# A gated block's third pair started a round later, the second expert block's groups cut 4, 2, 2, and the dealing begun with the lead-in round

## The chip, the cores and the metric

The kernel runs on one core of one Trainium2 chip. The metric is the device time of one execution in microseconds (us); of several runs the median is given. Engines are named as the profile names them: PE multiplies matrices (PEld is its weight loading), DVE and ACT work elementwise, POOL issues the row scatters and small powers, SP issues the plain DMAs.

## The reference

Eight sequences of 512 positions and 128 channels go through a chain of blocks, each added to its input after a layer norm. What matters here is the end of the chain:

```python
x = x + attention(layernorm(x))     # L1_attn_a, softmax over 16 heads
x = x + experts(layernorm(x))       # L1_ffn, first block ("m" in the kernel)
x = x + gated(layernorm(x))         # L1_attn_b, gated linear attention
x = x + experts(layernorm(x))       # L1_ffn again, second block ("n")

def experts(x):                     # top 2 of 8 experts per position
    xn = rms_norm(x)
    scores = xn @ w_router.T
    ids = top_k(scores, 2);  c = softmax(scores)[ids]
    h = val * silu(gate)            # val, gate = xn @ w_up[e].T, 352 wide each
    return sum(c * (h @ w_down[e].T)) + x
```

The gated block is a scan along the positions of one sequence, with projections, a short convolution, a series for a logarithm, and matrix products over chunks of 128 positions.

## The kernel before

**Expert blocks.** Positions are sorted by expert. A block works in *groups* of sequences (`GROUPS`, L26: one tuple for each block). For a group of `seqs` sequences there are 4 x `seqs` token tiles of 128 positions and `tiles_of(seqs)` slots of 128 rows: 39 for four sequences, 23 for two. The steps of a group are: `steps` (norms and router scores, for each sequence), `choose` (L1038 on: top 2, softmax, and for each row its slot; chains of small DVE instructions, with two matmuls at L1073 and L1074), scatters of the rows to `slots` in DRAM (L1159, one for each token tile and choice), `tiles` (L1189 on), scatters of the results to `given` (L1171, one for each slot tile), and `combine` (L1296 on: loads of `y` from `given`, and `add`, whose weighted additions into `x` are L1324).

The scatters are dealt by the generator `posts`, one at each call; it prefers rows to `slots` unless five results wait. A group's first load from `slots` waits for all its scatters, and a `y` load waits for all of the group's results.

A slot tile in `tiles` is: two products with `w_up` (L1274, L1275), a tanh on ACT (L1280), two multiplications on DVE (L1287, L1288), three transposes (L1238), their copy (L1240), the product with `w_down` (L1247) and its copy to `yr` (L1250). Four slot tiles share one load (`xr`, L1207) and one transposing step `turned` (L1218, L1220). `tiles` yields once after the first loads and then once for each slot tile and two more: a group of 39 takes 42 such *pieces*.

**Gated block.** It works on four *pairs* of sequences. `gated_steps` (L1573 on) cuts a pair's work into 25 steps, to which four steps of the second expert block's norms and scores are added (`steps` in `gated_and_experts`). `pipeline` (L54) runs the pairs in *rounds*. A round is the list `ages` of 29 places; an entry a means "the next step of the pair that started a rounds ago". There are 2 places with age -1 (the norm; places 15 and 22), 15 with age 0 (the first transposes L1630 to the product at L1768), 8 with age 1 (chunk products from L1776 to the sum into `x`, L1845) and 4 with age 2 (the expert norms and scores). So a pair's first step is its norm in the round ahead of its own, and round -1 holds the norm of pair 0 alone.

**What is dealt beside the pairs.** After each place from round `first` on, `pipeline` takes one step of `side`, a table of streams and the steps at which each is called (`dealt`). `at(now, places)` gives the steps `(now + 1) * 29 + place`. In the table `first` and `last` are the first block's two groups, `before.tiles(last)` the 42 pieces of its second group, `posts` its scatters; `one`, `two` and `three` are the second block's groups, `own` its scatters, and `tiles` their pieces one group after the other. After the rounds `run(side)` calls what is left of the table, and then `blend` runs the remaining pieces (`left`), scatters and combines in the *tail*.

The order in which the program is written is the order in which PE, DVE, ACT and POOL run it (`in_program_order`); only scatters of one set are loose among themselves.

Of the kernel before, what the change touches and what calls it, by code (L numbers as in the profile page):

```python
# [20 lines left out]
B = 8  # L21
# [1 line left out]
D = 128  # L23
NT = S // P

GROUPS = ((4, 4), (2, 4, 2))  # L26
MOST = max(max(g) for g in GROUPS)


# [24 lines left out]
def pipeline(make, count, ages, side=None, every=0, first=0):  # L54

    live = {}
    done = 0
    for now in range(min(ages), count + max(ages)):  # L60
        for age in ages:
            n = now - age
            if 0 <= n < count:
                if n not in live:
                    live[n] = make(n)
                next(live[n], None)
            done += 1
            if side is not None and now >= first and done % every == 0:
                next(side, None)
# [5 lines left out]
@contextmanager  # L75
def in_program_order(tc, *loose):


    block = tc.nc.cur_bb
    first = len(block.bb.instructions)  # L80
    yield
    assert tc.nc.cur_bb is block
    engines = (mybir.EngineType.PE, mybir.EngineType.DVE, mybir.EngineType.Activation, mybir.EngineType.Pool)
    last = {}
    for i in block.bb.instructions[first:]:
        if i.engine in engines:
            group = next((one[i.name] for one in loose if i.name in one), None)
            before = last.setdefault(i.engine, {})
            for other, names in before.items():
                if group is None or other != group:  # L90
                    for name in names:
                        tc.add_manual_dep(i, name, ORDER, reason="the order in which it is written")
            if group is None:
                before.clear()
            before.setdefault(group, []).append(i.name)
# [805 lines left out]
def blend(*streams):  # L901


    live = [[iter(one), 0, n] for one, n in streams]
    while live:
        one = min(live, key=lambda l: (l[1] + 1) / l[2])
        one[1] += 1
        if next(one[0], live) is live:
            live.remove(one)
# [426 lines left out]
def run(stream):  # L1336
    for _ in stream:
        pass


def fast(stream, *many):

    while True:
        for n in many:
            for _ in range(n):
                if next(stream, stream) is stream:
                    return
            yield


def idle(many):
    yield from range(many)
# [10 lines left out]
def until(true):  # L1363

    while not true():
        yield


def whole(stream):

    for _ in stream:
        pass
    yield


def dealt(*streams):

    streams = [(iter(stream), set(steps)) for stream, steps in streams]
    for q in range(1 + max(max(steps) for _, steps in streams)):
        for stream, steps in streams:  # L1380
            if q in steps:
                next(stream, None)
        yield
# [7 lines left out]
def in_turn(m):  # L1391


    streams = [(m.tiles(g), turns(g) - (g.number > 0)) for g in m.groups]

    def pieces():
        for i, (stream, n) in enumerate(streams):
            for at in range(n):
                if at == n - 3 and i + 1 < len(streams):
                    next(streams[i + 1][0])  # L1400
                next(stream)
                yield

    return pieces(), sum(n for _, n in streams)
# [75 lines left out]
def gated_and_experts(k, before, posts, slots, keep, banks, out):  # L1480

    tc = k.tc
    first, last = before.groups
    with tc.tile_pool(name="moe1", bufs=1, side="right") as room:
        m = Experts(k, "n", slots, keep, room, before.p3, out)
        m.hids = before.hids
        one, two, three = m.groups
        tiles, pieces = in_turn(m)
        own = m.posts(sum(2 * g.n + g.tiles for g in m.groups))
        with tc.tile_pool(name="gla1", bufs=1) as alone, tc.tile_pool(name="gla", bufs=2) as pool:  # L1490
            with k.banks(**banks["gated"]):
                gated = gated_steps(k, alone, pool)

                def steps(pair):
                    yield from gated(pair)
                    for _ in zip(m.steps(2 * pair), m.steps(2 * pair + 1)):
                        yield

                ages = (0, 0, 1, 0, 1, 1, 0, 2, 1, 1, 0, 2, 0, 2, 0, -1, 1, 0, 2, 0, 0, 1, -1, 0, 1, 0, 0, 0, 0)

                def at(now, *places):
                    return [(now + 1) * len(ages) + i for i in places]

                side = dealt(  # L1510
                    (before.tiles(last), at(-1, 4, *range(7, 29)) + at(0, *range(0, 29, 2)) + at(1, *range(4))),
                    (posts, at(-1, *range(29)) + at(0, *range(29)) + at(1, *range(6))),
                    (posts, at(-1, *range(9))),
                    (whole(posts), at(1, 6)),
                    (before.combine(first), at(-1, *range(9, 18))),
                    (before.combine(last), at(1, *range(8, 15), 17, 19)),
                    (m.choose(one), at(2, *range(19, 29)) + at(3, *range(3))),
                    (own, at(3, *range(3, 29)) + at(4, *range(29)) + at(5, *range(32))),
                    (own, at(5, *range(0, 32, 2))),
                    (tiles, at(3, *range(20, 29, 2)) + at(4, *range(0, 29, 4)) + at(5, *range(0, 32, 4))),  # L1520
                    (fast(m.choose(two), 2), at(4, *range(19, 26))),
                    (m.choose(three), at(5, *range(19, 32))),
                )
                with in_program_order(tc, before.loose, m.loose):
                    pipeline(steps, B // 2, ages, side=side, every=1)
                    run(side)
        with k.banks(**banks["experts"]), in_program_order(tc, m.loose):
            left = pieces - 21

            def combined(g):  # L1530
                yield from until(lambda: len(g.back) == g.tiles)
                yield from idle(3)
                yield from m.combine(g)

            blend((tiles, left), (take(fast(own, 1, 2), left), left), (chain(*(combined(g) for g in m.groups[:2])), left))
            run(own)
            run(m.combine(three))
# [556 lines left out]
def net_kernel(ctx: ExitStack, tc: tile.TileContext, drams, offsets, out):  # L2094
# [38 lines left out]
    w_a.close()  # L2133
    slots = [blank_slots(k, one) for one in GROUPS]
    with k.banks(**usual):
# [40 lines left out]
    with tc.If(large > 0):  # L2176
        nc.sync.dma_start(flat, saved)
        slots = [blank_slots(k, one) for one in GROUPS]
        again = ExitStack()
# [228 lines left out]
```

## Time and profile before

| | |
|---|---|
| median of 3 runs | 2065.78 us (2059.05 to 2067.45) |
| the profiled execution | 2068.02 us |
| its span | 2066.3 us |
| mean granted TensorE clock | 0.903 of full |
| busy: PE, PEld, DVE, ACT, POOL | 85%, 57%, 62%, 46%, 35% of the span |

A stretch of the profile is read by its window: the busy time of each engine in it, with the number of instructions in brackets, and the TensorE clock that was granted there. Matmuls are pipelined and their ends are modelled, so a PE that is busy all the time may still be below its peak. Durations are those of one execution. Some matmul records can be missing.

### The profile page before, as it was taken

How to read it: one execution, taken by the hardware profiler on the slowest of the kernel's cores; microseconds unless marked ns; L12 is line 12 of the kernel's file. 1: busy time of each engine (PE TensorE's matmuls, PEld its weight loads, DVE VectorE, ACT ScalarE, POOL GpSimd, SP SyncE). 2: the span in 40 equal slices, each digit the busy share in tenths (PEclk: the TensorE clock that was granted, in tenths of full speed). 3: DMA queues.
4: the chain of work that ended last, by engine and by line, in shares of the span. 5: the costliest groups of instructions: out<-in, count | busy, mean ns of one | idle time of the engine just before them, and what ended most of it. 6: DMA issues, size and time to landing. Idle time of an engine off the chain costs nothing. (4 is left out here: it accounts for less than half of the span.)

```text
span 2066.3 us, 29976 instructions
## 1 busy us (share of the span) xinstructions
PE 1751.9 (85%) x10171; PEld 1184.3 (57%) x10171; DVE 1287.4 (62%) x4211; ACT 943.7 (46%) x1703; POOL 731.0 (35%) x866
## 2 busy tenths in 40 slices
PE   4998789999998698899998878868898886847995
PEld 2655577887876455344444446645565654635774
DVE  7644888888886763565667456335746766434554
ACT  1022556666654322465555544434545553413553
POOL 2111333333333521344443663632212103355532
PEclk9898899999998888899999889978999787878998
DMA  9800000000000200000000021121101000112332
GB/s 256 148 1 1 0 1 1 1 1 1 1 1 1 90 1 41 1 1 1 1 1 1 22 70 36 54 75 43 32 10 33 21 1 12 47 41 69 93 103 65
DMA packets 79390, 71.25 MB, mean 34 GB/s; under 512 B 6560, under 2 KB 73120, under 8 KB 78336
## 3 DMA queue, kind: packets, MB, share of 16 engines
q1 hardware_dynamic: 69120, 47.89, 9.3%
q0 software_dynamic: 9536, 20.47, 3.0%
q8 instruction: 86, 1.41, 0.3%
q10 hardware_dynamic: 576, 0.90, 0.1%
q14 instruction: 72, 0.59, 0.1%
HBM read 34.98 MB, written 34.25 MB: 34 GB/s over the span
## 5 line engine op out<-in xcount | busy, mean ns | idle before, releaser
L165 POOL TENSOR_TENSOR ln_rs<-rs_v,mhalf 128x4 f32<-128x4 f32 x144 | 150.8, 1048 | 431.2 <-DVE rs_v L164 418.6
L1171 POOL DMA_INDIRECT given<-yr,to x163 | 160.0, 982 | 345.6 <-ACT yr L1250 105.5
L1287 DVE SCALAR_TENSOR_TENSOR half<-half,ps_a 128x352 f32<-128x352 f32 x163 | 84.6, 519 | 222.8 <-ACT half L1280 179.7
L679 ACT ACTIVATE pr<-ps_s 128x1024 f32<-128x1024 f32 x160 | 154.7, 1018 | 120.8 <-PE ps_s L669 120.7
L1275 PE MATMUL ps_a<-w_m,xt 128*128 x326 | 135.3, 499 | 34.8 <-DVE half L1287 22.4
L1274 PE MATMUL ps_a<-w_m,xt 128*128 x326 | 137.2, 505 | 19.8 <-ACT xt L1220 7.9
L1159 POOL DMA_INDIRECT slots<-xn,rpos x128 | 124.7, 974 | 74.2 <-issue 35.6
L669 PE MATMUL ps_s<-qm,rot 32*128 32x128 f32 (+3 forms) x1024 | 124.8, 490 | 23.6 <-ACT pr L679 23.5
L683 POOL TENSOR_SCALAR_AFFINE_SELECT pr<-pr 128x256 f32<-128x256 f32 x256 | 100.2, 416 | 111.5 <-ACT pr L679 107.2
L530 PEld LDWEIGHTS ps_c<-w_e,mlp_g 128*128 128x128 f32 x1024 | 126.6, 198 | 15.1 <-issue 14.8
L1240 ACT COPY gt<-ps_b 128x384 f32<-128x384 f32 x163 | 78.1, 479 | 112.9 <-PE ps_b L1238 85.2
L530 PE MATMUL ps_c<-w_e,mlp_g 128*128 128x128 f32 x1024 | 128.8, 281 | 0.1
L522 PE MATMUL ps_a<-zt,w_e 128*128 128x512 f32 x256 | 123.7, 607 | 0.9 <-ACT zt L211 0.9
L1280 ACT ACTIVATE half<-ps_a 128x352 f32<-128x352 f32 x163 | 75.9, 466 | 90.3 <-PE ps_a L1274 73.4
L1275 PEld LDWEIGHTS ps_a<-w_m,xt 128*128 128x128 f32 x326 | 63.7, 204 | 83.9 <-DVE half L1287 32.8
L178 DVE BATCH_NORM_AGGREGATE ln_mv<-ln_st 128x2 f32<-128x6 f32 x576 | 100.3, 179 | 16.3
L669 PEld LDWEIGHTS ps_s<-qm,rot 32*128 32x128 f32 x1024 | 60.2, 195 | 82.2 <-ACT pr L679 55.6
L523 ACT ACTIVATE mlp_g<-ps_a,w_col 128x512 f32<-128x512 f32 x128 | 85.8, 687 | 35.4 <-PE ps_a L522 35.4
L224 POOL TENSOR_TENSOR xe<-xe,w_erow 128x512 f32<-128x512 f32 x64 | 82.3, 1306 | 55.2 <-DVE ks L480 54.9
L1238 PEld LDWEIGHTS ps_b<-w_ident,hid 128*128 128x128 f32 x489 | 63.7, 147 | 65.0 <-issue 29.4
L373 ACT ACTIVATE mlp_g<-ps_a,w_col 128x512 f32<-128x512 f32 x64 | 44.0, 687 | 123.9 <-PE ps_a L372 123.2
L1288 DVE SCALAR_TENSOR_TENSOR hid<-half,ps_a 128x352 f32<-128x352 f32 x163 | 85.0, 521 | 18.8 <-PE ps_a L1274 1.1
(385 smaller groups left out, 4054.3 us busy)
## 6 DMA issues: line engine op xcount, KB each, us to landing
xr<-slots SPq DMA_DIRECT2D x37, 260.0 KB
y<-given SPq DMA_DIRECT2D x32, 256.0 KB
slots<-blank SPq DMA_DIRECT2D x3, 2535.0 KB
w_m<-in_m_dram SPq DMA_DIRECT2D x2, 2244.0 KB
w_e<-in_e_dram SPq DMA_DIRECT2D x2, 1700.0 KB
slots<-blank SPq DMA_DIRECT2D x2, 1495.0 KB
given<-yr,to POOLq DMA_INDIRECT x163
x<-in_u_dram SPq DMA_DIRECT2D x8, 256.0 KB
```

Of the source, the lines that this page charges most:

```text
L165: nc.gpsimd.tensor_tensor(out, v, self.mhalf[:, :n], ALU.pow)
L178: nc.vector.bn_aggr(mv[:, t, :], st[:, t, :])
L522: nc.tensor.matmul(ph, w1[:, c * P : (c + 1) * P], ht, start=True, stop=True)
L523: nc.scalar.activation(g[:, c, :], ph, AF.Relu, bias=col["e_b1"][:, l, c : c + 1])
L530: nc.tensor.matmul(py[:, t, :], g[:, c, t * P : (t + 1) * P], w2[:, c, :], start=(c == 0), stop=(c == 3))
L669: nc.tensor.matmul(halves[g // 2][:, g % 2, at : at + S - u * P], kr[rows, u * P : (u + 1) * P], qm[rows, i, u * P : S], start=True, stop= ...
L679: nc.scalar.activation(pr, sc, AF.Exp)
L683: nc.gpsimd.affine_select(out=v, in_=v, pattern=[[0, 2], [1, P]], compare_op=ALU.is_ge, fill=0.0, base=0, channel_multiplier=-1,)
L1159: made = nc.gpsimd.indirect_dma_start(out=g.slots, out_offset=bass.IndirectOffsetOnAxis(ap=g.pos[:, i, t : t + 1], axis=0), in_=g.xn[:, t, :],
L1171: made = nc.gpsimd.indirect_dma_start(out=g.given, out_offset=bass.IndirectOffsetOnAxis(ap=to, axis=0), in_=yr, in_offset=None,)
L1274: nc.tensor.matmul(pg, xt, w["experts"][:, bass.ds(o + HID, HID)], start=True, stop=True)
L1275: nc.tensor.matmul(pv, xt, w["experts"][:, bass.ds(o, HID)], start=True, stop=True)
```

## The change

- `GROUPS` for the second block goes from (2, 4, 2) to (4, 2, 2) sequences: 39, 23 and 23 slot tiles in place of 23, 39 and 23. Group `one` then holds pairs 0 and 1, `two` pair 2, `three` pair 3.
- `pipeline` takes a list of rounds in which pairs start. Pairs start in rounds 0, 1, 3 and 4 in place of 0, 1, 2 and 3, so there is one round more.
- `first=-1`: the dealing begins with round -1 in place of round 0. `at(now, ...)` therefore falls in round `now`; before it fell in round `now + 1`.
- The table of what is dealt is written anew.

By rounds as they run (p0a1 is pair 0 at age 1; places in brackets where they matter):

| round | pairs before | dealt before | pairs after | dealt after |
|---|---|---|---|---|
| -1 | p0a-1 | nothing | p0a-1 | 17 pieces of `last` (4, 7 to 22), `combine(first)` (9 to 17) |
| 0 | p0a0, p1a-1 | 23 pieces of `last`, `combine(first)` (9 to 17) | p0a0, p1a-1 | 15 pieces of `last` |
| 1 | p1a0, p0a1, p2a-1 | 15 pieces of `last` | p1a0, p0a1 | 10 pieces of `last` |
| 2 | p2a0, p1a1, p0a2, p3a-1 | 4 pieces, `combine(last)` (8 to 19) | p1a1, p0a2, p2a-1 | `combine(last)` (3 to 11) |
| 3 | p3a0, p2a1, p1a2 | `choose(one)` (19 to 28) | p2a0, p1a2, p3a-1 | `choose(one)` (19 to 25), 3 calls of `own` |
| 4 | p3a1, p2a2 | end of `choose(one)`, 26 calls of `own` (16 scatters of `one` are there), 5 pieces of `one` | p3a0, p2a1 | 29 calls of `own` |
| 5 | p3a2 | 29 calls of `own`, 8 pieces, `choose(two)` | p3a1, p2a2 | 29 calls of `own`, 15 pieces of `one`, `choose(two)` |
| 6 | none | 48 calls of `own`, 8 pieces, `choose(three)` (32 steps, no pair left) | p3a2 | 32 calls of `own`, 16 pieces, `choose(three)` |
| tail | | 71 pieces | | 61 pieces |

Pair 0's norm has its first step at place 15 of round -1. Before, it stands ahead of all adds of `combine(first)`; after, it stands behind those for the pair's two sequences. The same holds for the norms of the other three pairs: ahead of the adds for their sequences before, behind them after.

```diff
-GROUPS = ((4, 4), (2, 4, 2))
+GROUPS = ((4, 4), (4, 2, 2))
...
-    for now in range(min(ages), count + max(ages)):
+    starts = {start: n for n, start in enumerate(range(count) if isinstance(count, int) else count)}
+    for now in range(min(ages), 1 + max(starts) + max(ages)):
         for age in ages:
-            n = now - age
-            if 0 <= n < count:
+            n = starts.get(now - age)
+            if n is not None:
...
                 side = dealt(
-                    (before.tiles(last), at(-1, 4, *range(7, 29)) + at(0, *range(0, 29, 2)) + at(1, *range(4))),
-                    (posts, at(-1, *range(29)) + at(0, *range(29)) + at(1, *range(6))),
+                    (before.tiles(last), at(-1, 4, *range(7, 23)) + at(0, *range(0, 29, 2)) + at(1, *range(0, 28, 3))),
+                    (posts, at(-1, *range(29)) + at(0, *range(29)) + at(1, *range(29))),
                     (posts, at(-1, *range(9))),
-                    (whole(posts), at(1, 6)),
+                    (whole(posts), at(2, 1)),
                     (before.combine(first), at(-1, *range(9, 18))),
-                    (before.combine(last), at(1, *range(8, 15), 17, 19)),
-                    (m.choose(one), at(2, *range(19, 29)) + at(3, *range(3))),
-                    (own, at(3, *range(3, 29)) + at(4, *range(29)) + at(5, *range(32))),
-                    (own, at(5, *range(0, 32, 2))),
-                    (tiles, at(3, *range(20, 29, 2)) + at(4, *range(0, 29, 4)) + at(5, *range(0, 32, 4))),
-                    (fast(m.choose(two), 2), at(4, *range(19, 26))),
-                    (m.choose(three), at(5, *range(19, 32))),
+                    (before.combine(last), at(2, *range(3, 12))),
+                    (fast(m.choose(one), 2), at(3, *range(19, 26))),
+                    (own, at(3, *range(26, 29)) + at(4, *range(29)) + at(5, *range(29)) + at(6, *range(32))),
+                    (tiles, at(5, 0, *range(2, 29, 2)) + at(6, *range(0, 32, 2))),
+                    (fast(m.choose(two), 2), at(5, *range(19, 26))),
+                    (fast(m.choose(three), 2), at(6, *range(19, 26))),
                 )
                 with in_program_order(tc, before.loose, m.loose):
-                    pipeline(steps, B // 2, ages, side=side, every=1)
+                    pipeline(steps, (0, 1, 3, 4), ages, side=side, every=1, first=-1)
                     run(side)
...
-            left = pieces - 21
+            left = pieces - 31
```

## The prediction

> **What bounds the kernel now.** I read the busy times by stretch first, because the change touches only the time from about 1370 us to the end. The stretches were cut at the starts of the gated rounds, found in the timeline: the first transpose of each pair (L1630) starts at 1370.5, 1475.2, 1577.3 and 1648.2 us, so round 0 is 1370 to 1475, round 1 to 1577, round 2 to 1648, round 3 to 1731, round 4 to about 1780, round 5 to about 1805. Busy time by engine, then granted clock, DMA share and GB/s:
>
> ```profile
> core 0: us, PE busy (x) PEld busy (x) DVE busy (x) ACT busy (x) POOL busy (x), PEclk, DMA share, GB/s
> 1370.00:1475.00 105.00, 85.30 (x398) 56.55 (x399) 65.66 (x175) 53.80 (x109) 26.78 (x25) 0.87 0.20 57
> 1475.00:1577.00 102.00, 89.39 (x467) 61.63 (x465) 56.12 (x137) 48.65 (x95) 21.09 (x20) 0.90 0.04 13
> 1577.00:1648.00 71.00, 64.77 (x327) 43.65 (x327) 51.17 (x146) 38.60 (x68) 15.68 (x13) 0.83 0.12 36
> 1648.00:1731.00 83.00, 61.66 (x289) 39.80 (x287) 54.72 (x156) 35.48 (x59) 7.24 (x5) 0.80 0.00 1
> 1731.00:1780.00 49.00, 39.22 (x213) 29.68 (x214) 20.81 (x76) 16.75 (x33) 21.80 (x20) 0.75 0.15 44
> 1780.00:1805.00 25.00, 20.27 (x112) 16.16 (x111) 12.82 (x51) 14.10 (x35) 9.29 (x8) 0.86 0.12 33
> 1805.00:1878.00 73.00, 35.94 (x164) 25.86 (x163) 31.15 (x118) 15.63 (x38) 41.31 (x43) 0.74 0.16 51
> 1878.00:1990.00 112.00, 104.76 (x606) 80.14 (x605) 54.70 (x151) 56.80 (x141) 57.62 (x61) 0.97 0.25 74
> 1990.00:2042.00 52.00, 49.93 (x291) 37.29 (x291) 34.66 (x96) 28.32 (x68) 18.60 (x20) 1.00 0.34 100
> ```
>
> PE is the nearest engine to full everywhere, so its idle time is what a new order can win: 20 us in round 0, 13 in round 1, 6 in round 2, 21 in round 3, 10 and 5 in rounds 4 and 5, and 37 of 73 us from 1805 to 1878, at a clock of 0.74. Then I asked where the expert tiles lie, by the tanh that each has once (L1280):
>
> ```profile
> 1648.00:1731.00 83.00, 0.00 (x0) 0.80 0.00 1
> 1731.00:1780.00 49.00, 1.39 (x3) 0.75 0.15 44
> 1780.00:1805.00 25.00, 2.77 (x6) 0.86 0.12 33
> 1805.00:1878.00 73.00, 5.12 (x11) 0.74 0.16 51
> 1878.00:1990.00 112.00, 19.67 (x42) 0.97 0.25 74
> ```
>
> From 1805 to 1878 only 11 tiles run, 6.6 us each, where the tail makes 42 in 112 us, 2.67 us each. The longest waits of that stretch (us in total, times, longest):
>
> ```profile
> DVE half L1287 <- ACT half L1280: 23.0, 6, 14.9
> PEld ps_b L1073 <- issue: 17.0, 2, 13.9
> PE ps_b L1073 <- DVE rt L1067: 13.5, 1, 13.5
> ```
>
> L1073 is the matmul inside `choose`: PE comes to it late, and the tiles behind it on PE and DVE, dealt every fourth place, come later still.
>
> **Prices from these rows.** PE time of a tile: 104.76/42 = 2.5 and 49.93/22 = 2.3, so 2.4 us. Age 0, 1 and 2 of a pair: round 4 has 39.2 us of PE with 3 tiles (7), which leaves 32 for age 1 and age 2, taken as 28 and 4. Round 3 (one of each age, no tile) has 61.7, so age 0 is 30. Check: round 0 has age 0 and 23 tiles, 30 + 55 = 85, measured 85.3.
>
> **The change, part by part.** All the work stays: 163 tiles, 128 scatters, the same adds. What moves is who runs beside whom, and one round is added. I add up the new rounds, each from the start of its first instruction, beginning like the old at 1370.
>
> *Round -1* (16 tiles, four adds of `combine(first)`, pair 0's norm). The last scatter of `last` is issued at 1367.5 in both. In the second block the way from the last scatter (1765.5) to the first tile's tanh (1774.3) took 8.9 us, so the first tile's tanh comes at about 1376, against 1388 before. PE is uncovered there, since pair 0's steps, which filled 1370 to 1386, now come later. The y loads took 4.1 us for four, issued when the last rows of `given` have landed, early in the round; the 16 adds wanted by place 15 (0.35 us each, L1324) and the norm, 4 us of DVE, fit beside tiles whose two multiplications are 1.04 us. New wait: pair 0's norm stands behind those adds in DVE's order, and the tiles' multiplications behind both; I add 2 us. SP's later loads of y wait for the adds (four buffers), with loads of xr queued behind them; these are two fours ahead, so nothing. 6 + 16 x 2.4 + 2 = 46 us; from 43 to 59, the upper end by 3.3 us a tile, the rate of the first block's first group (1228 to 1358, 39 tiles).
>
> *Round 0* (age 0, 15 tiles): PE 30 + 36 = 66, plus the 13 us that PE idles in the old round 0 after 1393 (82 less 68.64 busy): 79, from 68 to 90.
>
> *Round 1* (age 0, age 1, 10 tiles): the old round 1 had 16 tiles in 102 us with PE 88% busy; six fewer give 88, from 82 (PE alone) to 95.
>
> *Round 2* (age 1, age 2, `combine(last)`, no tile): in the old round 4 the age 1 of pair 3 took from 1731 to 1768 (end of L1837) before tiles began. 37, plus half of 11 us of adds on DVE, plus 3 for a lower clock: 46, from 37 to 56. The last `given` post to the first y took 7 us before (1594.4 to the load's end at 1601.8); here the first add has the steps of places 2 to 5 in front of it, 11 us in the old round 4: hidden.
>
> *Round 3* (age 0 of pair 2, age 2 of pair 1, `choose` of a group of 16 tiles of tokens, no age 1). I walk the chain of age 0: first transposes to silu 15 us (1370.5 to 1385.8, with no tile beside it), then per step as in rounds 0 to 3 with waits for company left out: 5, 9, 5, 3, 4, 3 and 8. 52 in all. `choose` stretched the end of age 0 by 8 us (from its eleventh to last step, 21 in round 2, 29 in round 3) for a group of 8 token tiles; for 16 I take 12. Age 2 and the next norm, 11 us on DVE, fall mostly in DVE's waits: 4. With 2 for the clock: 70, from 60 to 83 (all of the old round 3).
>
> *Round 4* (age 0, age 1, 29 of the 32 scatters): the old round 3 less `choose` (8) and age 2 (4): 71, from 66 to 83. The scatters go at 1.27 us apart, 41 us of POOL; the small powers on POOL (L165) queue among them, one scatter deep: nothing.
>
> *Rounds 5 and 6* (age 1 and two ages 2, 31 tiles, two `choose`): PE 28 + 4 + 36 = 68 plus 3 for the first load and 4 for `choose` is 75; 4 + 38 plus 3 is 45. Together 120, from 112 to 140. The cover here is the tiles themselves; if the scatters were late, PE would stand at place 2.
>
> The clock is weighed at rounds 2 to 4. The rows show 0.97 to 1.00 where tiles follow each other and 0.74 to 0.83 where PE idles. I have put 3 + 2 us into the sum for it. The Trainium skill, "TensorE: Matmul & The Clock Gate", section "HAM oscillation — how this bites in real kernels", says that PE gaps beyond about 3.4 us put the clock to half; the trace agrees in direction (0.74 in the emptiest stretch); by that rule at work throughout rounds 2 to 4 the sum would be rival 1's 2082, by the rows 2054.
>
> *Tail.* Before: 65 tiles from 1877.5 (the 21st tile of the first group) to 2042.5, then 24 us of last combine. Ten tiles fewer: 165 - 24 + 24 = 165, from 155 to 172.
>
> Sum: 46 + 79 + 88 + 46 + 70 + 71 + 120 + 165 = 685 from 1370, a span of 2055 against 2066.3: 11 us less. The profiled run took 2068.0 us, 2 over the median of 2065.8, so the median becomes **2054 us**. A measurement of this kernel tells about 0.5%, 10 us, from no change.
>
> **The rivals.**
>
> 1. *The emptied rounds run cold (slower).* Rounds 2 to 4 hold no tile. Then PE idles, its clock falls, and each PE step on the chain stretches. For it: 0.75 to 0.80 in the old rounds with none. If round 2 takes the old round 4's 49, and rounds 3 and 4 the old round 3's 83, that is 215 instead of 187: 2054 + 28 = **2082**. It decides once the three exceed 208. Against: the old round 2, with only 3 tiles, kept PE 91% busy. Chance 0.22.
>
> 2. *The lead-in doesn't run at the tail's rate (no change).* With adds and norm in DVE's order the 16 tiles go at 3.0 us: +10, **2064**. For it: the first group's 3.3 us. Against: the tail has adds too and made 2.4. The wish of the change, cover for 1805 to 1878, is then paid in front. Chance 0.11.
>
> 3. *The rounds end sooner (faster).* Rounds 3 and 4 overlap, since the next pair's transposes start before the last steps (7 us in round 2 to 3), and PE in rounds 0, 5 and 6 is nearly full: 60 + 66 + 72 + 112 in place of 70 + 71 + 79 + 120 is 30 less: **2024** to 2035. Chance 0.15.
>
> 4. *The work is only carried along (no change).* The 31 tiles in rounds 5 and 6 replace 20, but if they go at 3 us instead of 2.4 the gain of 11 is gone by 19: **2066** to 2073. For it: six of them took 25 us in the old round 5. Against: 1.0 clock once tiles are dense. Chance 0.07.
>
> **How the numbers follow.** The forecast has 0.45, with its own range 2042 to 2066: 0.31 of it faster by over 0.5% (below 2055), 0.14 within. Rival 3 adds 0.15 to faster: 0.46. Within: 0.14 + 0.11 + 0.05 of rival 4 = 0.30. Slower: 0.22 + 0.02 = 0.24. The range takes in most of rivals 1 and 3: 2028 to 2084.
>
> **What would show it.** Right: tile tanhs from about 1376 on every 2.4 us; rounds 2 and 3 near 46 and 70 us; round 5 from about 1770; 30 tanhs of the second block from there to about 1890, 4 us apart, then 2.4 us apart to the end; PE busy over 85% from 1770 to 2030. Wrong: rounds 2 to 4 together over 208 us at a clock under 0.75, tiles of rounds 5 and 6 over 3 us apart, or the first tile later than 1385.

## The result, and the profile after

| | before | after |
|---|---|---|
| median of 8 runs each | 2065.27 us (2059.05 to 2069.39) | 2054.23 us (2041.95 to 2057.45) |
| ratio, 95% interval | | 0.9943 (0.9925 to 0.9961) |
| the profiled execution | 2068.02 us | 2054.95 us |
| its span, mean granted clock | 2066.3 us, 0.903 | 2053.0 us, 0.904 |

The change is worth 11 us. A second comparison, the same two kernels as the runs f1 and f2 below, gave 0.9915 (0.989 to 0.994), 16 us. The forecast was 2054.

In the profile after, the lines of the kernel stand one further down: the tanh L1280 is L1281, the products are L1275 and L1276, the multiplications L1288 and L1289, the scatters L1160 and L1172, the loads L1208, the adds into `x` L1325. Behind the table of what is dealt it is two (L1845 is L1847). The rounds were cut as before, at the first transposes of a pair where one starts, otherwise at the first step of the oldest pair. Rounds -1 to 6 take the first eight windows. The ninth runs from the 31st tanh of the second block to the last, and the tenth is the final combine. Busy time by engine, granted clock, DMA share and GB/s of the kernel after:

```profile
core 0: us, PE busy (x) PEld busy (x) DVE busy (x) ACT busy (x) POOL busy (x), PEclk, DMA share, GB/s
1370.00:1420.60 50.60, 42.49 (x214) 31.68 (x215) 31.98 (x106) 21.48 (x51) 16.45 (x17) 0.82 0.37 104
1420.60:1500.40 79.80, 66.44 (x313) 43.50 (x312) 47.05 (x116) 44.09 (x88) 18.42 (x18) 0.91 0.07 20
1500.40:1583.60 83.20, 71.16 (x384) 47.93 (x383) 45.10 (x91) 39.05 (x72) 15.08 (x14) 0.91 0.03 9
1583.60:1625.80 42.20, 30.93 (x183) 24.57 (x184) 26.96 (x99) 13.36 (x26) 8.42 (x8) 0.73 0.18 54
1625.80:1680.10 54.30, 41.35 (x128) 23.15 (x129) 38.11 (x132) 29.20 (x51) 8.07 (x7) 0.69 0.00 1
1680.10:1756.80 76.70, 58.13 (x260) 35.27 (x258) 47.02 (x96) 29.96 (x46) 36.56 (x35) 0.78 0.09 28
1756.80:1834.50 77.70, 66.24 (x377) 50.60 (x378) 40.61 (x148) 32.94 (x71) 17.45 (x17) 0.87 0.13 35
1834.50:1891.90 57.40, 45.90 (x253) 35.36 (x253) 32.19 (x125) 26.75 (x69) 32.34 (x33) 0.91 0.19 55
1891.90:2029.30 137.40, 128.49 (x752) 96.71 (x751) 76.30 (x208) 71.61 (x176) 66.62 (x70) 1.00 0.31 89
2029.30:2053.00 23.70, 3.74 (x27) 2.88 (x25) 6.46 (x20) 2.19 (x6) 4.79 (x5) 0.65 0.29 84
```

The emptiest stretch of before (1805 to 1878, PE busy 36 of 73 us) has no counterpart: in rounds 5 and 6 PE is busy 112 of 135 us. In exchange rounds 2 to 4 are thin now, 130 of 173 us at a clock of 0.69 to 0.78. The tanh of the expert tiles (one for each) in the same windows, those without a tile left out:

```profile
core 0: us, ACT busy (x), PEclk, DMA share, GB/s
1370.00:1420.60 50.60, 6.94 (x15) 0.82 0.37 104
1420.60:1500.40 79.80, 8.57 (x17) 0.91 0.07 20
1500.40:1583.60 83.20, 3.69 (x8) 0.91 0.03 9
...
1756.80:1834.50 77.70, 6.46 (x14) 0.87 0.13 35
1834.50:1891.90 57.40, 7.41 (x17) 0.91 0.19 55
1891.90:2029.30 137.40, 25.14 (x55) 1.00 0.31 89
```

15 tiles run in the lead-in round, where before there were none, 31 run in rounds 5 and 6, and the tail makes 55 in 137.4 us, 2.5 each.

**Where the time came from.** PE's work is the same in both kernels, so the difference is in its idle time. I cut both traces at three events that each kernel has: the last scatter to `slots` of group `last`, the last addition of the last pair into `x` (L1845 before), and the 31st tile of the second block. Before:

```profile
core 0: us, PE busy (x) PEld busy (x) DVE busy (x) ACT busy (x) POOL busy (x), PEclk, DMA share, GB/s
1367.50:1777.70 410.20, 338.46 (x1678) 230.19 (x1679) 246.37 (x678) 192.07 (x359) 93.54 (x84) 0.84 0.10 30
1777.70:1909.90 132.20, 86.45 (x427) 64.23 (x427) 59.12 (x214) 44.68 (x110) 66.92 (x68) 0.81 0.16 48
1909.90:2066.30 156.40, 130.57 (x778) 99.60 (x776) 82.78 (x228) 73.78 (x181) 64.69 (x68) 0.94 0.30 88
```

After:

```profile
core 0: us, PE busy (x) PEld busy (x) DVE busy (x) ACT busy (x) POOL busy (x), PEclk, DMA share, GB/s
1367.40:1827.20 459.80, 370.54 (x1823) 251.73 (x1823) 271.67 (x768) 207.56 (x395) 120.10 (x112) 0.83 0.11 32
1827.20:1891.90 64.70, 52.10 (x283) 40.33 (x282) 37.36 (x144) 29.26 (x74) 34.66 (x36) 0.89 0.18 52
1891.90:2053.00 161.10, 132.23 (x778) 99.59 (x776) 82.77 (x228) 73.80 (x181) 71.41 (x75) 0.95 0.30 88
```

PE is busy 555.5 us in the three parts before and 554.9 after. It idles 71.7 + 45.7 + 25.8 = 143 us before and 89.3 + 12.6 + 28.9 = 131 after. So the pairs run on for 50 us more and lose 18 us more beside them, the stretch behind the last pair shrinks by 68 us and loses 33 us less, and the end loses 3 more: 12.6 us net, of the 13.3 by which the spans differ. Which part of the change does this is what the experiments ask.

### The profile page after: what moved, and what is told of

Read it like the earlier page. It is cut to its first block, busy times and chain, and to the rows that moved or that the text cites. A ratio compares the mean times of both kernels' runs of the same rounds, so it can differ in the third digit from the quotient of the medians.

```text
span 2053.0 us, 29986 instructions
## 1 busy us (share of the span) xinstructions
PE 1752.7 (85%) x10171; PEld 1183.4 (58%) x10171; DVE 1288.2 (63%) x4211; ACT 943.9 (46%) x1703; POOL 729.3 (36%) x866
## 5 line engine op out<-in xcount | busy, mean ns | idle before, releaser
L1172 POOL DMA_INDIRECT given<-yr,to x163 | 158.5, 972 | 308.1 <-PE ps_a L1275 77.7
L1288 DVE SCALAR_TENSOR_TENSOR half<-half,ps_a 128x352 f32<-128x352 f32 x163 | 84.5, 519 | 198.0 <-ACT half L1281 166.3
L1276 PE MATMUL ps_a<-w_m,xt 128*128 x326 | 133.1, 491 | 25.1 <-DVE half L1288 13.2
L1160 POOL DMA_INDIRECT slots<-xn,rpos x128 | 125.3, 979 | 78.4 <-issue 26.4
L1275 PE MATMUL ps_a<-w_m,xt 128*128 x326 | 135.6, 500 | 5.4 <-ACT xt L1221 3.3
L1281 ACT ACTIVATE half<-ps_a 128x352 f32<-128x352 f32 x163 | 75.6, 464 | 103.3 <-PE ps_a L1275 92.7
L1276 PEld LDWEIGHTS ps_a<-w_m,xt 128*128 128x128 f32 x326 | 63.3, 202 | 72.2 <-DVE half L1288 20.9
L212 ACT ACTIVATE zt<-ps_b,w_col 128x512 f32<-128x512 f32 x80 | 62.6, 783 | 75.4 <-PE ps_b L205 75.4
```

What stands on the lines that cost most here:

```text
L1160: made = nc.gpsimd.indirect_dma_start(out=g.slots, out_offset=bass.IndirectOffsetOnAxis(ap=g.pos[:, i, t : t + 1], axis=0), in_=g.xn[:, t, :],
L1172: made = nc.gpsimd.indirect_dma_start(out=g.given, out_offset=bass.IndirectOffsetOnAxis(ap=to, axis=0), in_=yr, in_offset=None,)
L1275: nc.tensor.matmul(pg, xt, w["experts"][:, bass.ds(o + HID, HID)], start=True, stop=True)
L1276: nc.tensor.matmul(pv, xt, w["experts"][:, bass.ds(o, HID)], start=True, stop=True)
```

## The experiments

Each ratio is against the kernel before on the same chip, with its 95% interval. In the quoted expectations T is the theory that I held when the run was sent, or it is named by a letter of its own, and the others are its rivals; the question that a run puts is said in its first sentence. Runs e1 to e4 shared one chip (before: 2063.7 us, 17 runs), e5 to e8 a second (before: 2027.8 us, 29 runs), f1 to f4 a third (before: 2063.7 us, 22 runs).

For e1 to e3, and for f1 and f2 (the kernels before and after on the third chip), this table gives the same three parts as above (length, and PE's idle time in it):

| | last pair's last addition | 31st tile | end | PE idle in all |
|---|---|---|---|---|
| before | 410.2, idle 71.7 | 132.2, idle 45.7 | 156.4, idle 25.8 | 143 |
| after | 459.8, idle 89.3 | 64.7, idle 12.6 | 161.1, idle 28.9 | 131 |
| e1, before and early dealing | 445.8, idle 75.7 | 91.9, idle 30.4 | 155.7, idle 25.6 | 132 |
| e2, after without early dealing | 418.6, idle 87.3 | 115.3, idle 31.3 | 161.7, idle 30.1 | 149 |
| e3, after without the gap | 405.3, idle 70.8 | 114.7, idle 29.5 | 162.2, idle 29.1 | 129 |
| f1, before | 407.4, idle 72.7 | 132.2, idle 41.9 | 156.1, idle 25.2 | 140 |
| f2, after | 458.2, idle 89.2 | 64.7, idle 12.5 | 162.9, idle 29.4 | 131 |

Two things limit what this table can say. Each row is one execution, and executions differ already ahead of the first cut, where nothing was changed: the last scatter to `slots` of group `last` falls at 1360.8 us in e4 and at 1371.4 in e2, on one chip, and at 1371.7 in f1 and 1365.3 in f2. So 6.4 of the 16.3 us between the spans of f1 and f2 lie ahead of everything that was changed; from the cut on, the kernel before takes 698.8 and 695.7 us and the kernel after 685.6 and 685.8, 10 to 13 us less. And idle time isn't the whole account for e1 to e3: PE is busy for 562, 547 and 553 us there, against 555, so that they take 693.4, 695.6 and 682.2 us from the cut on.

**e1_lead_only** asks whether the early start of the dealing alone brings the gain. The kernel before, its own table, its groups (2, 4, 2), its pairs in rounds 0 to 3:

```diff
-                    pipeline(steps, B // 2, ages, side=side, every=1)
+                    pipeline(steps, B // 2, ages, side=side, every=1, first=-1)
```

> The kernel before with one part of the change alone: the dealing begins with the lead-in round (first=-1), with its own table, its own groups (2, 4, 2) and pairs in rounds 0 to 3. Theory T (the gain is the sum of rounds: PE idle time of the thin stretch after the last pair is filled, whoever fills it): the 22 tiles of the lead-in take about 65 us, every later round loses the tiles it had, and the thin stretch stays, because the two small groups of tiles still run alone at its end: about 2060, between 2050 and 2070. Rival R (the whole gain is the earlier start of the dealing; gap and groups are neutral): 2054 or less, the gain complete here.

Measured: 2053.45 us, 0.9959 (0.9943 to 0.9975). One argument in one line brings 0.41% of the 0.57% and 0.85% measured for the whole change; its interval reaches into that of the first of these two. The time lies within T's range and meets R's bound too, so this run alone doesn't decide between them. Its profiled execution was the slowest of six, 6 us over their median, and is only 2 to 5 us shorter from the cut on than the kernel before, so that the share of the early start is open. It shifts the whole table a round earlier, the second block's part too. The table shows the same trade in small: the pairs run on for 36 us more and lose only 4 more, and the stretch behind them falls by 40 us and loses 15 less.

**e2_no_lead** is the counterpart: the whole change, but the dealing begins in round 0, so that every entry of the new table falls a round later.

```diff
-                    pipeline(steps, (0, 1, 3, 4), ages, side=side, every=1, first=-1)
+                    pipeline(steps, (0, 1, 3, 4), ages, side=side, every=1)
```

> The changed kernel with the dealing begun with round 0 as before (first=0); groups, gap and table as changed, so that each entry falls one round later. Theory T: the first tile comes at about 1388 again, rounds 0 to 2 are fuller, the second block's 31 tiles lie in round 6 and after it: about 2060, between 2053 and 2072. Rival R: the gain is gone, 2065 or more.

Measured: 2064.25 us, 1.0005 (0.999 to 1.002). The time is in T's range and just short of R's bound; by the ratio the gain is gone, as R had it. Without the early start the gap, the new groups and the new table, its entries a round later, are together worth nothing. Behind the last pair PE loses 14 us less than before (31.3 for 45.7), beside the pairs 16 more (87.3 for 71.7): the gap only carries idle time from one side of the last pair to the other. With the early start (after) the part beside the pairs does 39 us more of PE work (370.5 for 331.3) at 2 us more of idle time.

**e3_no_gap** asks whether the gap is needed: the whole change, but pairs start in rounds 0, 1, 2 and 3.

```diff
-                    pipeline(steps, (0, 1, 3, 4), ages, side=side, every=1, first=-1)
+                    pipeline(steps, B // 2, ages, side=side, every=1, first=-1)
```

> The changed kernel with pairs in rounds 0, 1, 2 and 3 again; everything else as changed (pair 2's norm then stands ahead of the adds of the second group, as it did before). The last sixteen tiles dealt in rounds then run with no pair beside them. Theory T: the rounds cost what their load costs: round 2 with three ages 71, round 3 with three ages and choose 83, round 4 with two ages 44, round 5 48, the last tiles 47, where the changed kernel has 42, 54, 77, 78 and 57: 15 us less, about 2040, between 2030 and 2050. Rival G (the gap itself pays, because pairs that stand alone run at their own chain's speed): 2055 or more.

Measured: 2049.79 us, 0.9944 (0.9928 to 0.996): by its ratio level with the change itself, which was not run beside it, and at the upper edge of T's range. I had expected about 2040, because the rounds would be shorter, and they were: the last pair's last addition comes 54 us earlier after the last scatter than with the gap. But group `one` is not ready then. Its scatters end late, and the first tile's tanh comes only at 1785.7, 17 us after that addition. Busy times of e3 between the two, and the waits there (us in total, times, longest):

```profile
core 0: us, PE busy (x) PEld busy (x) DVE busy (x) ACT busy (x) POOL busy (x), PEclk, DMA share, GB/s
1768.50:1786.00 17.50, 2.98 (x7) 1.89 (x8) 0.94 (x6) 1.00 (x2) 7.18 (x8) 0.50 0.33 91
```

```profile
PEld ps_b L1219 <- issue: 16.3, 1, 16.3
PE ps_b L1219 <- DMA xr<-slots: 16.3, 1, 16.3
```

PE is idle for 14.5 of these 17.5 us, waiting for the first load from `slots`. So the gap is neutral: with it PE loses 18 us more beside the pairs (89.3 for 70.8) and 17 less behind them (12.6 for 29.5), since its thin rounds are the cover of the 32 scatters of a group of four.

**e4_groups_back** asks what the groups are worth: the new rounds and early start with groups (2, 4, 2). Fewer tiles can be dealt there, since the first group has 23.

```diff
-GROUPS = ((4, 4), (4, 2, 2))
+GROUPS = ((4, 4), (2, 4, 2))
...
-                    (tiles, at(5, 0, *range(2, 29, 2)) + at(6, *range(0, 32, 2))),
+                    (own, at(6, *range(0, 32, 2))),
+                    (tiles, at(5, 0, *range(2, 29, 2)) + at(6, *range(0, 14, 2))),
...
-            left = pieces - 31
+            left = pieces - 22
```

> The changed kernel with the second block's groups (2, 4, 2) again; since the group of four is then chosen after round 5, only 22 pieces can be dealt in the rounds, and 16 more scatters are called in round 6. Theory T: 9 tiles move from a round where each costs about 2.4 us of PE to the tail where each costs 2.5, and round 6 is left with 32 scatters at 1.27 us and little PE work: 5 to 15 us slower than the changed kernel, 2060 to 2070. Rival R: within 3 us of the changed kernel.

Measured: 2082.64 us, 1.0101 (1.0085 to 1.0118), 13 to 23 us more than I had expected. The group of four now comes second, and its 32 scatters fall behind the last pair. Busy times of e4 in that stretch, then its tanhs:

```profile
1846.00:1910.00 64.00, 29.63 (x108) 20.76 (x108) 19.18 (x90) 13.04 (x34) 45.60 (x46) 0.63 0.21 63
```

```profile
1846.00:1910.00 64.00, 2.31 (x5) 0.63 0.21 63
```

Five tiles in 64 us, PE 46% busy, POOL 71% busy with scatters that it issues 1.26 us apart. In this round order, and with this dealing, the groups (2, 4, 2) cost more than the change gains; no other dealing of them was tried here. That isn't true of every order: e1 has (2, 4, 2) and gains.

**e8_lead_no_tiles** asks what it is in the early start: tiles in the lead-in round, or everything else being earlier. The second block's table stays as in the change; the first block's pieces are dealt at every place of round 0 and every second of round 1, and the lead-in keeps only `combine(first)`, the calls of `posts` and the norm.

```diff
-                    (before.tiles(last), at(-1, 4, *range(7, 23)) + at(0, *range(0, 29, 2)) + at(1, *range(0, 28, 3))),
+                    (before.tiles(last), at(0, *range(29)) + at(1, *range(0, 26, 2))),
```

> The changed kernel with the 17 pieces of the lead-in round moved into rounds 0 and 1 (29 and 13 pieces); the lead-in keeps the scatters, the adds of the first group and the norm. It asks what the lead-in gives. Theory L (tiles must run in the lead-in, where PE has nothing else): round -1 shrinks to about 28 us, rounds 0 and 1 grow by about 33 and 7, so about 17 us slower, 2064 or more, ratio over 0.999. Rival P (what pays is that the table of side work stands a round earlier against the pairs; the tiles may lie anywhere): within 6 us of the changed kernel, ratio 0.992 to 0.997.

Measured: 2043.22 us, 1.0086 (1.0066 to 1.0106), on the second chip, where the change itself was not run. Its nearest neighbour there is e5 (below), which differs from the change by `choose(three)` alone: 1.0016. e8 is 13 us slower than e5, which fits theory L and not P. The lead-in, from the last scatter to pair 0's first transposes, in e8 and then in e5 (columns as above):

```profile
1356.30:1382.20 25.90, 0.03 (x1) 0.06 (x1) 13.64 (x53) 0.35 (x1) 6.83 (x7) 0.50 0.44 127
```

```profile
1355.30:1408.40 53.10, 42.45 (x214) 31.61 (x215) 31.95 (x106) 21.77 (x51) 18.39 (x19) 0.81 0.36 102
```

Without tiles PE stands idle for 26 us; with them it idles for 11 of 53. e8 pays for it in the rounds behind: when pair 2 starts, with the first block's work done in both, e8 is 267.2 us past the last scatter and e5 258.7. The first of the three parts, e8 and then e5:

```profile
1356.30:1824.60 468.30, 364.97 (x1823) 250.02 (x1823) 271.25 (x768) 207.94 (x395) 121.16 (x112) 0.83 0.11 31
```

```profile
1355.30:1818.40 463.10, 371.01 (x1823) 252.29 (x1823) 271.73 (x768) 207.97 (x395) 120.63 (x112) 0.83 0.11 32
```

The same 1823 matmuls, with 103 us of idle time in place of 92, but only 5.2 us longer, since e5 loses 5.9 us in round 4 to a wait that e8 doesn't have (below). The two later parts of e8 are 4.7 us longer than those of e5; in f2, which has `choose(three)` where e8 has it, they are 3.6 longer than in f3. So of the 13 us some 8 to 11, by these traces, hang on tiles being in the lead-in round, where nothing else fills PE; this is an estimate, since e8 also crowds rounds 0 and 1 and its neighbour isn't the change itself.

**e5_choose_in_tail and f3_choose_in_tail** are one kernel on two chips. They ask whether `choose(three)`, dealt in round 6 among the tiles, is what makes round 6 longer than forecast: it is dealt into the tail instead.

```diff
-                    (fast(m.choose(three), 2), at(6, *range(19, 26))),
...
-            blend((tiles, left), (take(fast(own, 1, 2), left), left), (chain(*(combined(g) for g in m.groups[:2])), left))
+            blend((tiles, left), (take(fast(own, 1, 2), left), left), (chain(*(combined(g) for g in m.groups[:2])), left), (m.choose(three), 90))
```

> The changed kernel with choose(three) taken out of round 6 and dealt into the tail, a step for each of its first dozen pieces. It asks why round 6 took 57 us where 45 were forecast. Theory C (the DVE chain of choose, and PE's wait for its matmul, stand between the tiles): round 6 goes to about 47 us and the tail grows by less, 2 to 6 us gained in all. Rival N (the norms and scores of the last pair, in the order of DVE and ACT, are what stretches it): round 6 stays within 3 us of 57, the total within 3 us or slower by as much as the tail's choose costs.

> The changed kernel with choose(three) dealt into the tail, once more, now beside the changed kernel itself. Theory C (the chain of choose stretches round 6): 2 to 10 us less than the changed kernel of this call. Rival N (the last pair's norms and scores stretch it): within 2 us or slower.

Measured: e5 2030.40 us, 1.0016 (1.0001 to 1.0032); f3 2051.26 us, 0.994 (0.9919 to 0.9962), beside 2047.78 of the change on f3's chip. By f3's profile against f2's, the stretch behind the last pair is 5.9 us shorter (58.8 for 64.7) and the end 2.3 longer, so about half of what round 6 took too long is `choose(three)`, as theory C had it. It does not come out as time: f3 is 3.5 us slower than the change where C had it 2 to 10 faster, because of a new wait. On e5's chip the change was not run, so e5 doesn't decide by its time. The DVE timeline of f3 in round 4 (start, duration; in brackets the idle time and who ended it):

```profile
1745.86 0.16 DVE L1747 COPY g_end<-cum 128x4 f32<-128x4 f32 x1
1752.34 0.18 DVE L1055 TENSOR_SCALAR xn<-w_m 128x8 f32<-128x8 f32 x1 [6.32 <-DMA slots<-xn,rpos]
```

The first instruction of `choose(three)` (L1055) now stands in round 4 in DVE's order. It writes into `xn`, DVE waits there until scatters out of `xn` have landed (group `one`'s are under way then), and so it stands for 6.3 us in the middle of the last pair's chain; e5 waits 5.9 us at the same instruction. Why the instruction moved up there is open.

**e6_scatter_early** asks whether the gap can be dropped with profit if the scatters are dealt faster (theory S), so that the wait seen in e3 is gone: e3, and in round 4 a second call of `own` at every other place, with tiles from place 18 of that round.

```diff
+                    (own, at(4, *range(0, 29, 2))),
-                    (tiles, at(5, 0, *range(2, 29, 2)) + at(6, *range(0, 32, 2))),
+                    (tiles, at(4, *range(18, 29, 2)) + at(5, *range(0, 29, 2)) + at(6, *range(0, 20, 2))),
```

> The kernel with pairs in rounds 0 to 3 and all else as changed, now with a second call of the scatters at every other place of round 4 and the 31 pieces of the second block begun at place 18 of round 4 in place of round 5. Without this its first tile of the second block came at 1786, 17 us after the last pair's sum into x (1769), with PE idle between. Theory S (without the gap, what was won in the rounds was given back as a wait for the group of four's 32 scatters, 1.27 us each): the first tile comes at about 1772, total 8 to 14 us less, ratio to before about 0.989. Rival D (the tiles that run alone are slowed by choose and the small scatters whatever their start): within 4 us of the kernel without it, ratio 0.993 to 0.996.

Measured: 2029.02 us, 1.0004 (0.9989 to 1.0019). The wait went as expected: the first tile's tanh comes at 1774.0, before the last pair's last addition (1784.2). The time did not: e6 is level with the kernel before, and with e5 on the same chip (1.0001 to 1.0032), which has the gap. e3 was not run on this chip, so what the faster scatters are worth against it isn't shown.

**e7_best and f4_best**, again one kernel on two chips, put the best together by theory S: e6 with the first block's part of the table as before the change (22 pieces in the lead-in, so that the four pieces and `combine(last)` in round 1 fit rounds without a gap), and `choose` of the second and third group a round earlier.

```diff
+                    (before.tiles(last), at(-1, 4, *range(7, 29)) + at(0, *range(0, 29, 2)) + at(1, *range(4))),
+                    (posts, at(-1, *range(29)) + at(0, *range(29)) + at(1, *range(6))),
...
+                    (whole(posts), at(1, 6)),
...
+                    (before.combine(last), at(1, *range(8, 15), 17, 19)),
...
+                    (fast(m.choose(two), 2), at(4, *range(19, 26))),
+                    (fast(m.choose(three), 2), at(5, *range(19, 26))),
```

> A candidate made of the parts so far: dealing from the lead-in round with the table of before for the first block (22 tiles in the lead-in), pairs in rounds 0 to 3, groups 4, 2, 2, scatters doubled in round 4, tiles from place 18 of round 4, choose(two) in round 4 and choose(three) in round 5. Theory S: the early chooses take the last chains away from the tiles that run alone: 2025 to 2040, ratio 0.982 to 0.989. Rival D: no better than the kernel with early scatters alone, 0.990 or more.

> The candidate once more (no gap, 22 tiles in the lead-in, groups 4, 2, 2, scatters doubled in round 4, both late chooses a round earlier), beside the changed kernel itself: theory S has it 10 to 18 us below the changed kernel of this call; if the tiles that run alone are slow whatever their start, within 5 us of it.

Measured: e7 2023.76 us, 0.9988 (0.9974 to 1.0002); f4 2053.23 us, 0.9946 (0.9923 to 0.9969). f4 is 5 us behind the change on the same chip, where theory S had it 10 to 18 ahead, so theory S falls; e7, too, is outside its range of ratios (0.982 to 0.989). f4's three parts are 436.2 us with 89.5 of idle time, 89.6 with 11.9, and 163.4 with 31.2: against f2 (458.2 with 89.2; 64.7 with 12.5; 162.9 with 29.4) the same idle time in other places, 133 and 131 us. Neither version that ran beside the change (f3, f4) beat it.

**f1_before and f2_after** are the two kernels of this case on the third chip.

> The kernel before itself, profiled again beside three others on one chip. Between two chips its median differed by 36 us (2063.7 and 2027.8), and four kernels whose stages after 1367 us took 670 to 686 us stood level with it on the second. If the chip changes only what all kernels share (theory A), its stretch from the last scatter of the first block to the end is about 699 us again, as in the first profile. If the chip changes this kernel more than the others (theory B: its thin stretch after the last pair depends on the chip), the stretch is about 675 us where the total is near 2028.

> The changed kernel itself, on the same chip as the three others of this call. Theory A: ratio to before 0.992 to 0.997 whatever the chip. Theory B: on a chip where before takes about 2028, ratio 0.998 to 1.008; where it takes about 2064, 0.992 to 0.997.

Measured: f1 2063.70 us, 0.999 (0.9973 to 1.0007), so that a kernel against itself comes out within 0.3%; f2 2047.78 us, 0.9915 (0.989 to 0.994), a little under the range that both theories gave for such a chip. f1's stretch from the last scatter on is 696 us, near theory A's 699. But this chip is one on which the kernel before is slow, so theory B wasn't put to the test.

## Why the prediction was right, and where it was not

The time was right (2054 forecast, 2054.2 measured), and so was its sum (685 forecast from 1370 on, 683 measured), but the terms were not all right, and the reason that I gave for the gain was only partly right. That the sum came out within 2 us is in part luck: round 3 missed by 16 us one way and round 6 by 12 the other, and the smaller misses cancelled too.

| term | forecast | measured |
|---|---|---|
| round -1 | 46 | 50.6 |
| round 0 | 79 | 79.8 |
| round 1 | 88 | 83.2 |
| round 2 | 46 | 42.2 |
| round 3 | 70 | 54.3 |
| round 4 | 71 | 76.7 |
| rounds 5 and 6 | 75 + 45 | 77.7 + 57.4 |
| tail | 165 | 161.1 |

*Round -1* held in its mechanism: the last scatter is issued at 1367.4, the first tanh comes at 1376.6 (forecast "about 1376"), and the next ones 2.2 to 3.1 us apart. The new wait that I put at 2 us was mis-sized. Timeline of the kernel after (start, duration, engine, line, operation; in brackets the idle time and who ended it):

```profile
1395.40 2.74 DVE L1325 SCALAR_TENSOR_TENSOR x<-y,m_c,x 128x128 f32<-128x128 f32 x8
...
1398.06 0.29 DVE L178 BATCH_NORM_STATS2 ln_st<-x 128x6 f32<-128x128 f32 x1
...
1398.58 0.46 ACT L1281 ACTIVATE half<-ps_a 128x352 f32<-128x352 f32 x1 [0.33 <-PE ps_a L1275]
...
1401.65 0.51 DVE L1288 SCALAR_TENSOR_TENSOR half<-half,ps_a 128x352 f32<-128x352 f32 x1
...
1402.85 0.90 PE L1239 MATMUL ps_b<-w_ident,hid 128*128 128x128 f32 x3 [3.69 <-DVE hid L1289]
...
1407.10 0.46 ACT L1281 ACTIVATE half<-ps_a 128x352 f32<-128x352 f32 x1 [0.48 <-PE ps_a L1275]
```

Between two tanhs lie 8.5 us in place of 2.4: eight adds of `combine(first)`, and behind them the norms of pair 0 (from 1398.06), stand on DVE ahead of the multiplications of the two tiles whose tanhs came at 1396.4 and 1398.6. PE waits 3.7 us for `hid`, then its products run at half pace (L1248 1.49 us for six, where 0.83 is seen six us earlier). 6 us, not 2.

*Round 3* was the largest miss, 16 us. The chain of age 0 was sized rightly: from the first transposes of pair 2 to the end of its age 0 (L1768 before) it took 66 us, 1625.8 to 1692.1. But the next pair starts 12 us before that end. That is the overlap of rival 3, which I had priced as a case of its own and left out of the sum. Rounds 3 and 4 together took 131 us: 10 less than the sum's 141, and 5 more than the rival's 126. Its other half, a fuller PE in rounds 0, 5 and 6, did not come (79.8 and 135 us for its 72 and 112).

*Round 6* failed the other way, 12 us over. The term took 16 tiles at 2.4 us plus 4 and 3; 17 fell into the window. The waits of the kernel after in that window (us in total, times, longest) show what was missing:

```profile
DVE half L1288 <- ACT half L1281: 11.1, 6, 4.1
ACT half L1281 <- PE ps_a L1275: 9.2, 8, 3.6
...
PEld ps_b L1025 <- ACT half L1281: 3.4, 1, 3.4
```

DVE waits for a tanh that stands on ACT behind four activations of the last pair's expert norm (L1019), and PE's transposes of that norm (L1025) wait in turn behind it:

```profile
1854.21 1.63 ACT L1019 ACTIVATE x<-x,m_nm,m_up 128x128 f32<-128x128 f32 x4
1855.75 0.44 ACT L1281 ACTIVATE half<-ps_a 128x352 f32<-128x352 f32 x1
1856.22 0.52 DVE L1288 SCALAR_TENSOR_TENSOR half<-half,ps_a 128x352 f32<-128x352 f32 x1 [4.12 <-ACT half L1281]
1856.60 1.11 PE L1025 MATMUL ps_b<-w_ident,xn 128*128 128x128 f32 x4 [3.12 <-ACT half L1281]
```

f3 put about 6 of the 12 us down to `choose(three)`, of which 2 came back at the end. The rest is argued from these lines and was not tried by itself. Rounds 5 and 6 thus made 31 tiles at 4.4 us, near the 4 that I named as a sign of being right, but also over the 3 that I named as a sign of being wrong: these two signs contradict each other. The two rounds took 135 us where the sum had 120, and round 6 kept PE 80% busy, not over 85%.

*Rounds 1, 2 and the tail* came out 4 to 5 us under their terms, round 4 six over, all within their ranges. I did not take these apart.

*Rival 1* (rounds 2 to 4 run cold) had its sign but not its price. The clock did fall, to 0.73, 0.69 and 0.78, in two of the three rounds below the 0.75 to 0.80 that I had set beside this rival. (I had misread two rows there: the 0.75 is of old round 4, which had three tiles, and old round 2 had two tiles, not three. Neither enters the price.) But the three rounds took 173 us, less than the sum's 187 and far from the 208 at which it decides. The Trainium skill, "TensorE: Matmul & The Clock Gate", section "HAM oscillation — how this bites in real kernels", says that gaps of some 3.4 us make PE slow and that this is paid as time; the trace agrees in direction with the first half (0.69 where PE is 76% busy). The second half does not show in the length of these rounds, which ended 14 us sooner than my sum with its 5 us for the clock; but the overlap of rounds 3 and 4 shortened them at the same time, so what the low clock cost isn't measured.

*Rival 2* (the lead-in is slow) gave 4 to 5 of its 10 us. *Rival 4* (tiles carried along at 3 us or more) was nearer than its chance: 4.4 us for each of the 31, but with the pair's own work beside them.

*The reason.* I had read the gain off the stretch 1805 to 1878 and credited the rounds' new order and the groups with filling it, with the lead-in as one more round that costs 46 us. The runs turn this round. The early start alone, in the old order, gains 0.41% (e1), the rest without it nothing (e2), the gap is neutral (e3), and without tiles in the lead-in some 8 to 11 us are lost (e8). The thin stretch is indeed filled, but filling it by the gap costs as much idle time in rounds 2 to 4. What pays is that the lead-in, in which PE had no work before the first pair's chain, takes 15 tiles, and that the work behind them comes earlier against the pairs. Those who count only the round that looks empty credit the wrong edit. The evidence for this comes from two chips, e1 to e3 from one and e8 from another, and on e8's chip no version with the early start was faster than the kernel before (last section).

Still open: how much of the change's 0.57% to 0.85% the early start makes by itself (0.41% by e1's median, less by its one profile), and what the new groups and table add to it, since the intervals overlap; and whether the change is faster on the second chip at all (last section).

## What to carry to other kernels

When a list of work is dealt beside a serial chain, cut the traces at events that both kernels have and count the idle time of the bound engine in each part over the whole region: an order that fills one hole (46 us to 13 here) may open another (72 to 89). Begin the count at the last event ahead of the change: what lay before it differed by 10 us between executions on one chip here. Look first for rounds in which the chain has not begun yet, because work put there takes nobody's place. And when work is moved up in an in-order engine's program, look for what its first instruction waits for: one small DVE write that waited for scatters stood for 6.3 us here, and the whole gain was gone.

## What the runs showed of the hardware that was not expected

The chips differ by more than the change. The kernel before took 2063.7 us on the first and third chip and 2027.8 on the second, 1.7% less. The kernel of e5 and f3 took 2030.4 and 2051.3 us, that of e7 and f4 2023.8 and 2053.2. Part of it lies ahead of everything that was changed, where the first block's tiles run beside its scatters. The same window of the same program, e5 and then f3:

```profile
1285.00:1335.00 50.00, 49.47 (x292) 38.92 (x293) 25.16 (x65) 27.68 (x67) 35.03 (x37) 0.97 0.19 58
```

```profile
1285.00:1335.00 50.00, 41.27 (x238) 30.03 (x237) 19.50 (x51) 21.29 (x56) 30.99 (x34) 1.00 0.17 53
```

On the second chip PE gets through 292 matmuls in 50 us, on the third through 238, at no lower a granted clock (0.97 and 1.00). In f3 the longest waits there are DVE's for the tanh, 18.8 us in 8 times and up to 4.6, in e5 22.1 us in 20 times and up to 2.4: the tiles come in bursts. The chips are told apart by this stretch in every profile: from the first to the last of the 39 tanhs of the first block's first group it takes 106 to 108 us in e5 to e8, on the second chip, and 120 to 126 us in the ten other runs. What of the chip does this was not tried. Of the 18.4 us between the two spans 7 are there by the last scatter (1355.3 and 1362.5), the rest arises after it.

A ratio therefore holds for a chip. The versions with the early start gained 0.5 to 0.6% on the third chip (f3 0.994, f4 0.9946) and nothing on the second (e5 1.0016, e7 0.9988), and the intervals do not meet. The change itself was only run where the kernel before is slow.
